# Sending tokens to slots: a routed expert layer that computes 13 of its 16 experts only for the tokens that chose them

## The chip, the cores and the metric

The kernel runs on one core of a Trainium2 chip. The metric is device time in microseconds (us) of one execution, taken as the median of several runs. The profile shown below is one execution recorded by the hardware profiler. All data are float32. TensorE is called PE in the profile (its weight loads PEld), VectorE DVE, ScalarE ACT, GpSimd POOL, and the engine that issues the ordinary DMAs SP.

## The reference, cut to what matters

Two transformer layers run over 1024 tokens of 256 channels. Each half of a layer is `x = x + layernorm(f(layernorm(x)))`; the four `f` are softmax attention, a mixture of 8 experts, a gated linear attention with 16 heads, and the mixture that is changed here:

```
def L1_ffn(x, gate_weight, gate_up_weights, down_weights, shared_gate_up, shared_down):
    # x: 1024 x 256; 16 experts of inner width 176; the shared one has 352
    scores = softmax(x @ gate_weight.T)
    topk_weight, topk_idx = top_k(scores, 4)
    y = 0
    for e in range(16):
        w_e = sum(where(topk_idx == e, topk_weight, 0), axis=-1)
        y += w_e[:, None] * glu(x, gate_up_weights[e], down_weights[e])
    return y + glu(x, shared_gate_up, shared_down)

def glu(x, gate_up, down):
    g, u = split(x @ gate_up.T, 2)
    return (silu(g) * u) @ down.T
```

A token has a non-zero weight for 4 of the 16 experts only. Counted with the reference on its own inputs, the 16 experts are chosen by 263, 231, 231, 261, 269, 237, 265, 251, 290, 273, 234, 236, 233, 246, 294 and 282 tokens.

## The kernel before

The whole network is one program. `Net.__init__` runs `attention0`, `experts0`, `attention1` and `experts1` one after the other. The residual `x` and the sum `acc` of the running half layer stay in SBUF by token (8 tiles of 128 tokens, `TT = 8`), and the normalised input `hT` stays there by channel (2 chunks of 128 channels by 1024 tokens). Weights come through a pool of two buffers, `wpool`; `load_next` issues the next group's DMAs on SP.

`experts1` treats all 16 experts and the shared one as a single layer with 16 x 176 + 352 = 3168 inner rows. These rows are cut into tiles of up to 128 (25 tiles), in groups `L1F`: first the shared expert's 3 tiles, then 22 tiles in groups of five (`FG1 = 5`). For each tile and each half of the tokens (512 of them) `gated` makes two products of two matmuls each (`pg` and `pu`, L803), ACT takes Silu of the one (L805), and DVE multiplies (L806) into `mid`. A tile of a routed expert is then multiplied by the weights of its tokens (`weigh`, L867). These weights lie along the free axis, so the routing weights are transposed (L771, L772), written to DRAM (L789) and read back as a broadcast over the partitions (L1407). `down` multiplies `mid` with the down weights, one matmul of 256 columns for each tile of tokens and each tile of rows (`po`, L821), and adds to `acc` (L829). After the last group `turn_out` normalises `acc`, adds `x` and sends the result out (L183 to L188, L314, L317, L318).

`router1` (L1435 to L1444) makes the routing weights for all 8 tiles of tokens at once, from logits of 16 matmuls (`pl`, L780). Which token chose which expert plays no part in how much is computed: every expert runs over all 1024 tokens, and a weight of zero removes what was not chosen.

The instructions are put in order when the program is built. The written order gives the priority, and each engine then runs its list strictly in that order; an instruction may be moved ahead of others that are not expected to be ready. `pinned` (`keep_in_program_order`) forbids that for single instructions. The last pieces of the previous half layer (the transposes of `h` into `hT`, L259 and L260) are kept in the list `todo` and run between the first tiles of `experts1` by `catch_up`.

Of the kernel before, what the change touches and what calls it, by code (L numbers as in the profile page):

```python
# [8 lines left out]

F32 = mybir.dt.float32  # L10
AF = mybir.ActivationFunctionType
ALU = mybir.AluOpType
# [3 lines left out]
P = 128  # L16
T = 1024
# [14 lines left out]
E1, F1, TOP1 = 16, 176, 4  # L32
FR = E1 * F1
FS = 2 * F1
FALL = FR + FS
FG1 = 5

L1F = [(FR, FS)] + [(lo, min(FG1 * P, FR - lo)) for lo in range(0, FR, FG1 * P)]

# [10 lines left out]
class Net:  # L50
    def __init__(self, ctx, tc, a, out):
# [39 lines left out]
        with tc.tile_pool(name="late", reuse_waits="tile", bufs=1) as late:  # L91
# [9 lines left out]
            self.experts0()  # L101
        self.attention1()
        self.experts1()

# [93 lines left out]
    def turning(self, ps, tp, acc=None):  # L198
# [41 lines left out]
        yield  # L240
        h = self.row.tile([P, 2, D], F32, tag="h2", name="h")
        for i, x in enumerate(xs):
# [95 lines left out]
    def normed0(self, tts):  # L338

        nc = self.nc
        n = len(tts)
        mv = self.mv0[:, tts[0] : tts[0] + n, :]
        for i, tt in enumerate(tts):
            st = self.small.tile([P, 6], F32, tag="st", name="st")
            nc.vector.bn_stats(st, self.x[:, tt, :])
            nc.vector.bn_aggr(mv[:, i, :], st)
        ve, rsx = (self.small.tile([P, n], F32, tag=t, name=t) for t in ("ve0", "rsx0"))
        nc.vector.tensor_scalar(ve, mv[:, :, 1], 1.0 + EPS, EPS * EPS, ALU.mult, ALU.add)  # L350
        nc.gpsimd.tensor_tensor(rsx, ve, self.nhalf[:, 0:n], ALU.pow)
        xns = []
        for i, tt in enumerate(tts):
            xn = self.row.tile([P, D], F32, tag="h", bufs=6, name="xn")
            nc.vector.tensor_scalar(
                xn, self.x[:, tt, :], mv[:, i, 0:1], rsx[:, i : i + 1], ALU.subtract, ALU.mult
            )
            xns.append((tt, xn))
        return xns, rsx
# [14 lines left out]
    def project0(self, tt, ps, qk, va, rotate):  # L374
# [12 lines left out]

        ra = self.row.tile([P, 2 * H, ROT], F32, tag="ra", bufs=2, name="ra")
        rb = self.row.tile([P, 2 * H, ROT], F32, tag="rb", bufs=2, name="rb")
        cos = self.rope[:, tt, 0, :].unsqueeze(1).to_broadcast([P, 2 * H, ROT])  # L390
# [4 lines left out]
        if rotate is not nc.vector:  # L395
            turn = self.row.tile([P, 2 * H, ROT], F32, tag="rc", bufs=2, name="rc")
            nc.scalar.copy(turn, src[:, :, 0:ROT])
# [7 lines left out]
    def attention0(self):  # L405
# [3 lines left out]
        QT = TT // 2  # L409
        with ExitStack() as ctx:  # L410
            big = ctx.enter_context(tc.tile_pool(name="a_big", reuse_waits="tile", bufs=1))
            qkp = ctx.enter_context(tc.tile_pool(name="a_qk", reuse_waits="tile", bufs=2))
# [394 lines left out]

    def down(self, ps, pieces, first, hf=None, then=None, apart=False):


        nc = self.nc
        begin, end = (0, TT) if hf is None else (hf * TT // 2, (hf + 1) * TT // 2)
        units = [list(range(tt, tt + 2)) for tt in range(begin, end, 2)]
        if apart:
            units[-1:] = [[tt] for tt in units[-1]]
        for tts in units:
# [15 lines left out]

    def experts(self, ps, tmp, midp, groups, route, weigh, then, join=False):


# [9 lines left out]
        def gates(half, some=slice(None)):  # L845
            g, tiles, hf, mid = half
            if join and (g, hf) == (0, 0):

                for part in (slice(0, HALF // 2), slice(HALF // 2, HALF)):
                    for i, (wg, wu, right, m, row) in enumerate(tiles):  # L850
                        self.gated(ps, tmp, wg, wu, mid[0:m, i, :], m, hf, part)
                    if part.start == 0:
                        self.catch_up(ps, 3)
                return
            for i, (wg, wu, right, m, row) in list(enumerate(tiles))[some]:
                self.gated(ps, tmp, wg, wu, mid[0:m, i, :], m, hf)
                self.catch_up(ps, 2)
                if g > 1:
                    weight(half, i)
# [9 lines left out]
        def down(*parts):  # L869
# [6 lines left out]
            last = g == len(groups) - 1  # L876
            self.down(ps, pieces, g == 0, hf, then if last else None, join and last and hf == 1)
            if hf == 1:
# [25 lines left out]
        for g in range(2, len(groups)):  # L904
            tiles = groups[g]()
            if join and g == 3:
                self.shifted()
            for hf in range(2):
                half = start(g, tiles, hf)
                if join and g >= len(groups) - 2 and (g, hf) != (len(groups) - 2, 0):  # L910
                    gates(half)
                    if g == len(groups) - 1:
                        down(behind.pop(0), half)
                    else:
                        behind.append(half)
                    continue
                if g == len(groups) - 1 and hf == 1:
# [103 lines left out]
    def attention1(self):  # L1021
# [3 lines left out]
        with ExitStack() as ctx:  # L1025
# [346 lines left out]
            for h in range(H):  # L1372
                ahead = enter(h + 1) if h + 1 < H else iter(())
                for _ in attend(h):
                    next(ahead, None)
                for _ in ahead:
                    pass


    def experts1(self):  # L1380
        nc, tc, a = self.nc, self.tc, self.a
        with ExitStack() as ctx:
            one = ctx.enter_context(tc.tile_pool(name="d_one", reuse_waits="tile", bufs=1))
            midp = ctx.enter_context(tc.tile_pool(name="d_mid", reuse_waits="tile", bufs=4))
            tmp = ctx.enter_context(tc.tile_pool(name="d_tmp", reuse_waits="tile", bufs=3))
            wp = ctx.enter_context(tc.tile_pool(name="d_w", reuse_waits="tile", bufs=7))
            ps = ctx.enter_context(tc.tile_pool(name="d_ps", reuse_waits="tile", bufs=8, space=PSUM))

            wr = one.tile([P, KC, E1], F32, name="wr")
            nc.sync.dma_start(out=wr, in_=a["e1_wrT"].rearrange("(k p) e -> p k e", p=P))  # L1390
            spreads = {}

            def route():
                w = self.router1(one, ps, wr)
                yield
                spreads["all"] = self.in_dram("w1", self.by_token(one, ps, w, E1), E1)
                yield

            def weigh(lo, m):

                if lo >= FR:
                    return None
                if lo not in spreads:
                    t = wp.tile([P, T], F32, tag="w", name="w")
                    for e in range(lo // F1, (lo + m - 1) // F1 + 1):
                        p0, p1 = max(e * F1 - lo, 0), min((e + 1) * F1 - lo, m)
                        nc.sync.dma_start(  # L1407
                            out=t[p0:p1, :], in_=spreads["all"][e, :].partition_broadcast(p1 - p0)
                        )
                    spreads[lo] = t  # L1410
                return spreads[lo]

            def group(g):
                gT, uT, dT = self.loaded.pop(0)
                tiles = []
                begin, rows = L1F[g]
                for i in range(-(-rows // P)):
# [6 lines left out]
                    ))  # L1424
                return tiles

            groups = [lambda g=g: group(g) for g in range(len(L1F))]
            self.experts(ps, tmp, midp, groups, route(), weigh, self.turn_out, True)

    def router1(self, one, ps, wr):  # L1430
        nc = self.nc
        sh = [P, TT, E1]
        pl = self.logits(ps, wr, E1)
        top = one.tile([P, TT, 1], F32, name="top")
        nc.vector.tensor_reduce(top, pl, AX.X, ALU.max)  # L1435
        w = one.tile(sh, F32, name="w")
        nc.vector.tensor_tensor(w, pl, top.to_broadcast(sh), ALU.subtract)
        nc.scalar.activation(w, w, AF.Exp)
        tot = one.tile([P, TT, 1], F32, name="tot")
        nc.vector.tensor_reduce(tot, w, AX.X, ALU.add)  # L1440
        nc.vector.reciprocal(tot, tot)
        nc.vector.tensor_tensor(w, w, tot.to_broadcast(sh), ALU.mult)
        chosen = self.first_k(one, w, E1, TOP1)
        nc.vector.tensor_tensor(w, w, chosen, ALU.mult)  # L1444
        return w

# [20 lines left out]
def layout(inputs):  # L1467
# [5 lines left out]
    def swap(v):  # L1473
        return v.transpose(0, 2, 1)

    def by_channel(v):
# [11 lines left out]
    )  # L1488
    gu, sgu = i["L1_ffn_gate_up_weights"], i["L1_ffn_shared_gate_up"]
    arrays = {  # L1490
        "x": i["L0_attn_X"].reshape(T, D), "cpack": cpack, "rope": _rope_table(),
# [8 lines left out]
        "e1_wrT": i["L1_ffn_gate_weight"].T,  # L1500
        "e1_gT": np.concatenate([gu[:, :F1].reshape(FR, D), sgu[:FS]], axis=0).T,
        "e1_uT": np.concatenate([gu[:, F1:].reshape(FR, D), sgu[FS:]], axis=0).T,
        "e1_dT": np.concatenate(
            [swap(i["L1_ffn_down_weights"]).reshape(FR, D), i["L1_ffn_shared_down"].T], axis=0
        ),
    }
# [18 lines left out]
```

## Time and profile before

| What | Value |
|---|---|
| Median of 3 runs | 1280.89 us (1280.16 to 1281.85) |
| The profiled execution's own time | 1274.77 us |
| Its span, first to last instruction | 1272.7 us |
| First matmul of `experts1` | 997.8 us into the span |
| Mean granted TensorE clock | 0.990 |

The profiled execution is 6.1 us faster than the median of the runs, and 2.07 us of its own time lie outside the span. In the page's lines on groups, the columns are line, engine, operation, output and inputs, shapes, and number of instructions, then busy time in us and mean duration in ns, then the idle time before them and what ended it. In answers on windows, each row is a stretch of the span with the busy time of every engine (and its number of instructions in brackets), the granted clock as a share of full speed, the share of the 16 DMA engines' time, and GB/s. "SPq" marks the issue of a DMA.

### The profile page before, as it was taken

What the parts mean: (1) busy time and instruction counts of PE and PEld (TensorE: products, weight loads), DVE (VectorE), ACT (ScalarE), POOL (GpSimd) and SP (SyncE); (2) the same over time, 40 slices, a digit from 0 to 9 for tenths busy, and PEclk for the clock granted to TensorE, in tenths of its full rate; (3) what the DMA queues carried; (4) which work ended last, traced back from release to release, by engine and by line L of the source; (5) the groups of instructions that cost most, each with busy time, mean ns of one, the idle gap of its engine ahead of it and who ended that gap; (6) DMA issues with size and microseconds to landing.
All of it is one profiled execution on the core that took longest, in us unless ns stands there. A gap on an engine that the chain in (4) does not pass through costs nothing. (4 is left out here: it accounts for less than half of the span.)

```text
span 1272.7 us, 15799 instructions
## 1 busy us (share of the span) xinstructions
PE 1214.0 (95%) x6152; PEld 727.1 (57%) x6152; DVE 732.0 (58%) x1646; ACT 501.0 (39%) x926; POOL 127.8 (10%) x118
## 2 busy tenths in 40 slices
PE   7999999999999997999999999999998899999997
PEld 4533333324456564567676776677677557555655
DVE  5876767732542355776777777768585633333234
ACT  4266665664310114444445454444544221121011
POOL 3100000000000001112111111121212200000001
PEclk9999999999899999999999999999999999999999
DMA  6000000000033012102030202120211106523000
GB/s 196 1 1 1 1 1 1 1 1 1 1 127 106 0 42 60 53 34 81 28 108 29 80 34 75 34 75 34 75 34 36 62 1 172 157 78 128 18 25 33
DMA packets 38922, 64.41 MB, mean 51 GB/s; under 512 B 4776, under 2 KB 28552, under 8 KB 38848
## 3 DMA queue, kind: packets, MB, share of 16 engines
q1 hardware_dynamic: 38848, 63.41, 15.8%
q8 instruction: 48, 0.79, 0.3%
q14 instruction: 26, 0.21, 0.1%
HBM read 62.12 MB, written 1.28 MB: 50 GB/s over the span
## 5 line engine op out<-in xcount | busy, mean ns | idle before, releaser
L481 DVE TENSOR_REDUCE pm<-sc 128x1 f32<-128x512 f32 x256 | 163.1, 684 | 64.5 <-PE sc L545 43.2
L806 DVE TENSOR_TENSOR mid<-sg,pu 128x512 f32<-128x512 f32 (+2 forms) x85 | 56.7, 667 | 194.1 <-PE pu L803 190.7
L805 ACT ACTIVATE sg<-pg 128x512 f32<-128x512 f32 (+2 forms) x85 | 49.4, 581 | 280.9 <-PE pg L803 280.9
L545 PE MATMUL sc<-qTm,kT 32*128 32x512 f32 x512 | 151.4, 643 | 1.9 <-ACT pe L563 1.9
L574 ACT ACTIVATE pe<-sc 128x512 f32<-128x512 f32 x216 | 117.7, 595 | 67.9 <-PE sc L545 47.3
L476 PE MATMUL sc<-kT,qT 32*128 32x512 f32 x512 | 136.3, 638 | 1.6 <-ACT qT L435 0.8
L1144 ACT ACTIVATE sn<-pt,shift,rs 128x128 f32<-128x128 f32 x256 | 93.5, 469 | 106.8 <-DVE shift L1140 106.8
L1104 PE MATMUL px<-hT,w_l1a 128*128 128x512 f32 x256 | 125.4, 602 | 5.4 <-DVE y L1096 5.1
L1096 DVE SCALAR_TENSOR_TENSOR y<-px,cp,y 128x1023 f32<-128x1023 f32 (+5 forms) x102 | 123.5, 1213 | 3.9 <-ACT y L1090 3.8
L803 PE MATMUL pg<-hT,w_l1f 128*128 128x512 f32 (+3 forms) x212 | 95.7, 574 | 2.1 <-ACT hT L260 2.1
L803 PE MATMUL pu<-hT,w_l1f 128*128 128x512 f32 (+3 forms) x212 | 95.4, 573 | 0.0
L829 DVE TENSOR_TENSOR acc<-acc,po 128x512 f32<-128x512 f32 (+1 forms) x55 | 37.2, 676 | 94.0 <-PE po L821 94.0
L821 PE MATMUL po<-w_l1f,mid 128*128 128x256 f32 (+1 forms) x400 | 87.6, 379 | 0.0
L821 PEld LDWEIGHTS po<-w_l1f,mid 128*128 128x128 f32 (+1 forms) x400 | 76.0, 190 | 13.5 <-issue 3.3
L1139 POOL TENSOR_TENSOR rs<-ve,nhalf 128x8 f32<-128x8 f32 x32 | 52.3, 1636 | 300.6 <-DVE ve L1138 245.9
L532 PE MATMUL po<-pe,va 128*32 128x256 f32 (+1 forms) x872 | 79.7, 433 | 1.3 <-ACT oT L537 0.8
L545 PEld LDWEIGHTS sc<-qTm,kT 32*128 32x128 f32 x512 | 49.6, 185 | 54.2 <-issue 38.5
L1208 PE MATMUL pg<-hT,w_l1a 128*128 128x512 f32 x128 | 62.0, 610 | 7.3 <-DVE og L1324 5.6
L803 PEld LDWEIGHTS pu<-hT,w_l1f 128*128 128x128 f32 (+1 forms) x212 | 40.6, 191 | 46.1 <-issue 45.0
L532 PEld LDWEIGHTS po<-pe,va 128*32 128x32 f32 x872 | 18.0, 108 | 85.0 <-issue 75.3
L803 PEld LDWEIGHTS pg<-hT,w_l1f 128*128 128x128 f32 (+1 forms) x212 | 40.1, 192 | 43.7 <-issue 39.8
L803 PE MATMUL pg<-hT,w_l0f 128*128 128x512 f32 x128 | 62.8, 612 | 0.0
(212 smaller groups left out, 1876.6 us busy)
## 6 DMA issues: line engine op xcount, KB each, us to landing
spread<-rows SPq DMA_DIRECT2D x32, 512.0 KB, 4.6
w<-w SPq DMA_DIRECT2D x16, 512.0 KB, 5.8
w_l1f<-in_e_gT SPq DMA_DIRECT2D x4, 640.0 KB, 4.0
w_l1f<-in_e_uT SPq DMA_DIRECT2D x4, 640.0 KB, 5.3
w_l1f<-in_e_dT SPq DMA_DIRECT2D x4, 640.0 KB, 7.0
w_l0f<-in_e_wg SPq DMA_DIRECT2D x4, 512.0 KB, 6.1
w_l0f<-in_e_wu SPq DMA_DIRECT2D x4, 512.0 KB, 7.2
w_l0f<-in_e_wd SPq DMA_DIRECT2D x4, 512.0 KB, 8.1
```

What stands on the lines that cost most here:

```text
L476: nc.tensor.matmul(sc, raw[r, tt * P : (tt + 1) * P], kT[r, g, half(kh)], start=True, stop=True,)
L481: nc.vector.tensor_reduce(pm[:, tt, 2 * pair + i, kh : kh + 1], sc, AX.X, ALU.max)
L532: nc.tensor.matmul(po[0][rows(j), c], va[:, st, g * G + j, :], pe[j // 2][:, j % 2, c], start=(st == 0), stop=(st == TT - 1 and c.stop == ...
L545: nc.tensor.matmul(sc, kT[rows(j), g, st * P : (st + 1) * P], qm[rows(j), :], start=True, stop=True,)
L574: nc.scalar.activation(pe[pair][:, i, :], sc, AF.Exp, scale=scale)
L803: nc.tensor.matmul(p, w(k), self.hT[:, k, c], start=(k == 0), stop=(k == KC - 1))
L806: nc.vector.tensor_tensor(mid, sg, pu, ALU.mult)
L821: nc.tensor.matmul(po[:, i, :], left[:, at * P : (at + 1) * P], right, start=(n == 0), stop=(n == len(pieces) - 1),)
L1096: nc.vector.scalar_tensor_tensor(y[:, at:hi], px[:, at - j : hi - j], column(cw + 4 * h + 3 - j), y[:, at:hi], ALU.mult, ALU.add,)
L1104: nc.tensor.matmul(px[:, c], w[:, k, hh * DK : (hh + 1) * DK], self.hT[:, k, c], start=(k == 0), stop=(k == KC - 1),)
L1144: nc.scalar.activation(sn[:, n, :], pts[n // 4][:, n % 4, :], AF.Identity, scale=rs[:, n : n + 1], bias=shift[:, n : n + 1],)
L1208: nc.tensor.matmul(pg, wg[:, k, hh * DK : (hh + 1) * DK], self.hT[:, k, c], start=(k == 0), stop=(k == KC - 1),)
```

## The change

The last three routed experts and the shared one keep the old form: `FD = 352 + 3 x 176 = 880` rows, 7 tiles instead of 25. They are called the dense part here. The other 13 (`SP1 = 13`) go through slots:

- `ways`, run before `attention1`, fills constants with POOL. `empty`, called once for each head of `attention1`, issues DMAs on SP that clear the first 336 rows of each expert's slots and a table of sums, both in DRAM: 13 of 357 KB and 11 of 128 KB.
- `routed(hf)` runs the router for one half of the tokens. It also counts, with matmuls against a triangle of ones (`earlier`) and a matrix of ones, how many earlier tokens chose the same expert, and makes from that the slot of each token in each expert. Then POOL issues, for each tile of 128 tokens and each of the token's 4 choices, an indirect DMA that writes the tokens' rows (256 channels, 13 weights and an index: 1088 bytes) to their slots. These are 16 DMAs for each half.
- `crowded` finds whether an expert was chosen by more than 336 tokens, and loads the answer into a register of every engine. `tc.If` takes `to_slots` if none was, and `to_all` otherwise, which computes the 13 experts for all tokens.
- `to_slots` reads, for each expert, its 336 rows from the slots (`fetch`), transposes them on PE (`turn`), makes the gated products with 336 columns (`middle`) and the down products with tokens on the partitions, scaled by the routing weight (`out`). It then sends the result with three indirect DMAs of 112 rows that add to the table of sums in DRAM. The adds of an expert wait for those of the expert before (`behind`). The weights come three experts at a time (`load`). At the end the sums are read back, added to `acc`, and `turn_out` runs.

The diff, cut to its core:

```diff
-L1F = [(FR, FS)] + [(lo, min(FG1 * P, FR - lo)) for lo in range(0, FR, FG1 * P)]
+SP1 = 13
+CP, CT = 112, 3
+CAP = CP * CT
+FD = FS + (E1 - SP1) * F1
+FG1 = 4
+L1F = [(lo, min(FG1 * P, FD - lo)) for lo in range(0, FD, FG1 * P)]
...
+        with tc.tile_pool(name="route", reuse_waits="tile", bufs=1) as self.route:
+            self.ways()
+            self.attention1()
+            self.experts1()
...
+                if h >= 1:
+                    self.empty(h - 1)
...
+            def routed(hf):
...
+                for i in range(N):
+                    for j in range(TOP1):
+                        tt = hf * N + i
+                        sent = nc.gpsimd.indirect_dma_start(
+                            out=self.slots[:, :],
+                            out_offset=bass.IndirectOffsetOnAxis(
+                                ap=place[:, tt, j : j + 1].bitcast(U32), axis=0
+                            ),
+                            in_=self.hrow[:, tt, :], in_offset=None,
+                            bounds_check=SLOTS - 1, oob_is_err=False,
+                        )
...
+            routed(0)
+            group(1)
+            for i in range(FG1, len(tiles)):
+                gates(i, 0)
+                self.catch_up(ps, 2)
+            self.catch_up(ps, len(self.todo))
+            routed(1)
+            for i in range(FG1):
+                gates(i, 1)
+            full = crowded()
+            spreads()
+            for i in range(FG1, len(tiles)):
+                gates(i, 1)
+            self.shifted()
...
+            def to_slots():
...
+                for i in range(2):
+                    load(i)
+                    fetch(i)
+                turn(0)
+                for e in range(SP1):
+                    if e + 1 < SP1:
+                        turn(e + 1)
+                    middle(e)
+                    if e > 0:
+                        out(e - 1)
+                    if e + 2 < SP1:
+                        fetch(e + 2)
+                    if e > 0:
+                        if e % S3 == 0 and (e // S3 + 1) * S3 < SP1 :
+                            load(e // S3 + 1)
+                out(SP1 - 1)
+                got = self.hT.rearrange("p k t -> p (k t)").rearrange("p (t d) -> p t d", d=D)
+                for tp in range(TT // 2):
+                    tts = [2 * tp, 2 * tp + 1]
+                    v = got[:, 2 * tp : 2 * tp + 2, :]
+                    read = nc.sync.dma_start(
+                        out=v, in_=self.sums[2 * tp * P : (2 * tp + 2) * P, :].rearrange("(t p) d -> p t d", p=P)
+                    )
+                    behind(read, added[SP1 - 1])
+                    acc = self.acc[:, 2 * tp : 2 * tp + 2, :]
+                    nc.vector.tensor_tensor(acc, acc, v, ALU.add)
+                    self.turn_out(ps, tts)
...
+            with tc.If(full == 0, preferred_fallthrough_block=True) as fits:
+                to_slots()
+            with fits.Else():
+                to_all()
```

Inside `out(e)`, the part that sends:

```diff
+                    for i in range(CT):
+                        sent = nc.gpsimd.indirect_dma_start(
+                            out=self.sums[:, :],
+                            out_offset=bass.IndirectOffsetOnAxis(
+                                ap=xs[:, i, XID : XID + 1].bitcast(U32), axis=0
+                            ),
+                            in_=ys[:, i, :], in_offset=None, bounds_check=TRASH - 1,
+                            compute_op=ALU.add,
+                        )
...
+                        behind(sent, added.get(e - 1, ()))
```

The rows fetched for an expert (`xs`) have three buffers, their transposes (`xT`) two, and the weights of three experts (`sw`) two.

## The prediction

> **What bounds the kernel now.** I read the busy table first, then the stage around the change by windows and by groups, then the chain of waits for the pace of a matmul.
>
> ```profile
> PE 1214.0 (95%) x6152; PEld 727.1 (57%) x6152; DVE 732.0 (58%) x1646; ACT 501.0 (39%) x926; POOL 127.8 (10%) x118
> q8 instruction: 48, 0.79, 0.3%
> ```
>
> PE is the bound over the whole span. For the stage (busy us of PE, PEld, DVE, ACT, POOL; clock; DMA share; GB/s):
>
> ```profile
> 997.80:1265.50 267.70, 266.18 (x876) 162.47 (x876) 93.47 (x191) 47.87 (x85) 7.01 (x13) 0.99 0.26 76
> 1065.00:1070.00 5.00, 5.00 (x25) 4.38 (x24) 2.58 (x4) 1.01 (x2) 0.00 (x0) 1.00 1.04 224
> 8.00:16.00 8.00, 7.45 (x21) 4.32 (x22) 4.81 (x20) 2.47 (x8) 2.99 (x4) 1.00 1.00 308
> 500.00:510.00 10.00, 4.86 (x12) 2.17 (x12) 5.78 (x10) 4.57 (x6) 0.00 (x0) 0.83 0.37 94
> ```
>
> From the first gate matmul to the last down matmul PE lacks 1.5 us. POOL is free. The 16 DMA engines are full at 224 GB/s in the broadcasts, at 308 in plain loads. The pace, from the chain (start, length, items; each matmul has its load):
>
> ```profile
> 1030.30 3.48 PE pl L780 x32
> 1122.60 1.72 PE pu L803 x4
> 1124.32 8.63 PE po L821 x40
> ```
>
> A matmul of 512 columns takes 0.86 us (1.68 ns a column), one of 256 takes 0.431, and a short one 0.217, whatever its width. What ends the kernel and what the DMAs cost:
>
> ```profile
> 1267.22 0.43 DVE L183 BATCH_NORM_STATS2 st<-acc 128x6 f32<-128x256 f32 x1
> 1269.64 0.42 DVE L317 TENSOR_TENSOR x<-x,acc 128x256 f32<-128x256 f32 x1 [0.67 <-ACT acc L314]
> x<-in_x SPq DMA_DIRECT2D x4, 256.0 KB, 3.3
> out_y<-x SPq DMA_DIRECT2D x8, 128.0 KB, 1.7
> spread<-rows SPq DMA_DIRECT2D x32, 512.0 KB, 4.6
> ```
>
> And a row on order: DVE ran an L806 inside the router's chain, which is written ahead of it.
>
> ```profile
> 1037.04 0.41 DVE L755 TENSOR_TENSOR_SCAN nth<-within,eq 128x128 f32<-128x128 f32 x1
> 1037.59 0.69 DVE L806 TENSOR_TENSOR mid<-sg,pu 128x512 f32<-128x512 f32 x1
> 1038.19 0.29 DVE L759 TENSOR_TENSOR nth<-nth,more 128x128 f32<-128x128 f32 x1
> ```
>
> So waiting steps are passed by ready ones; I use this for PE's order below.
>
> **The change part by part.** *PE, before:* 25 tiles x 2 halves x 4 x 0.86 = 172.0; downs 8 x 25 x 0.431 = 86.3; logits 3.5, transposes 3.5: 265.3, which is the 266.2 of the window. *PE, dense part after:* gates 7 x 8 x 0.86 = 48.2; downs 8 x 7 x 0.431 = 24.2; logits 3.5; transposes 3.5; the counts, 9 matmuls for slots and 2 for the limit, 2.4. Sum 81.8. *PE, one expert in slots:* 6 transposes 1.3, 6 gate matmuls of 336 columns 6 x 0.565 = 3.4, 6 down matmuls 2.6: 7.3, times 13 is 94.6. PE's work falls from 266 to 176. The rest of the sum is what is given back.
>
> *Dense part, waits.* The 1.5 us stay. The register load makes every engine wait for `over`; no row shows one. Below, 0 (PE has queued work); above, 4; the smallest loads land in 1.6 to 2.6 us, so I take 2. Behind it on PE stand the last three tiles' gates, which nothing else needs early. The broadcasts of the routing weights: before, from the issue of the write (1056.0) to the fifth tile's weighting (1073.4) took 17.4 us, hidden behind unweighted work. Now 2.1 MB instead of 2.6 go the same way (14 us, and 2 for transposes and copies), and PE has 10.3 us of gates to cover it and one more of unweighted downs: 5 us of wait. The dense part ends at 997.8 + 81.8 + 1.5 + 2 + 5 = 1088; 1 for the branch makes 1089. The two routers' chains on DVE (22 small instructions of 0.2 to 0.4 each, about 6 us) and their four table loads on ACT (1.28 each) lie beside gates; without that cover they would cost some 9 us a half.
>
> *POOL's indirect DMAs.* The trace has none. Their issue time X is bounded below by SP's issue of a plain DMA (0.37 to 0.46 us), above by twice POOL's L1139 (1.64 us for 8 columns), that is 3.3[...]. Nearest in kind is a small POOL instruction: 0.2 (memset) to 0.7 (pow). The Trainium skill (DMA: Bandwidth & Descriptors, section on latency and other measured facts) puts the first byte of a POOL-issued DMA at about 1 us against 0.6 for SP's. I take 1.2. For the landing L of an add: below 1.7 (out_y), above 1.7 + 3.3 (a read ahead of the write). The same page's section on the anatomy of one DMA has 2.0 us fixed; with it the sum would be about 6 us shorter. I take 3.0. The 32 sends: half 0 from about 1025, half 1 from about 1045, 16 x 1.2 each, landed by about 1067; the first fetch (4 us, between 3.3 and 4.6) is in at 1071. PE reaches it at 1089: hidden, up to X of about 2.3. On POOL behind the sends stand only the register load and the adds; on SP the first fetch holds up `load(1)`, wanted three experts later.
>
> *The slots' loop.* Three limits for one expert: PE, 7.3; the chain of adds, 3X + L + 0.3 = 6.9; and the ring of three row buffers, since the fetch of expert e + 3 waits for the adds of e: fetch 4.3, transposes 1.3, copy 0.6, gates 3.4, Silu and product 1.2, downs 2.6, scaling 0.6, adds 6.6, together 20.6 for three experts, 6.9. Limits so close cannot be met at once: a step that comes back finds PE in another expert's step, on average half of a 1.3 to 3.4 us step. I add 0.8: 8.1 for an expert, 105.5 for 13, and 0.6 + 6.6 until the last adds have landed: 113. DVE (1.5) and ACT (2.6 per expert, from 0.45 and 0.38 a piece) are covered. DMA moves 1.3 to 1.7 MB per expert, 160 to 210 GB/s, within the 308; but 1.9 MB of weights stand three times ahead of fetches on SP's queue (6 us at 308, mostly covered): 4. Adds end at 1089 + 113 + 4 = 1206.
>
> *The tail.* Before, 7.2 us followed the last down matmul. Now nothing of the output can be normalised before the last add: read back 3.4, then four pairs of tiles on DVE, 3.1 each (L829 0.69, two each of 0.43, 0.18 and 0.43, two of 0.16) = 12.4, 1.5 of POOL and ACT for the last pair, 2.6 to the end of the output. 19.9: 1226. All engines then jump over `to_all`. The trace has no jump; instruction fetches are DMAs (q8), and the smallest land in 1.6 to 2.6: bounds 0 and 4, I take 2.
>
> *Attention.* 24 clearing DMAs on SP lie at 0.4 us of issue each in a queue that is mostly idle; 8 of 16 scans already wait for `spread`, 7.9 us in all, with PE losing 1.0 of it. `ways` is a dozen POOL constants (about 5 us) before POOL has work. Together 0 to 10; I take 2. The edits of pools and of `h`'s place cost nothing: no instruction is added.
>
> Sum: 1226 + 2 + 2 = 1230, against the span's 1272.7: 42.7 less, 1232 in its own time. The median stands 6.1 above that execution, so 1280.9 - 42.7 = 1238.
>
> **A rule against the change.** The window 500 to 510 shows a clock of 0.83 where PE was busy 4.86 of 10 us. The skill (TensorE: Matmul & The Clock Gate, The HAM clock gate) says that an idle window of about 3.4 us halves the clock until about as long a busy one. My gap per expert is 0.8 us: by rule nothing. If the loop takes 11 us, gaps reach 3.7, and the rule would put up to 3.6 us on each expert's 7.3 (up to 47 in all), the row's 0.83 only 1.5 (19). I take nothing in the main case, and let it widen the upper end.
>
> **The rivals.**
> *POOL's chain of adds becomes the bound* (slower). Each expert then costs 3X + L, the span is 1089 + 14 + 13(3X + L) + 28. Break-even is 3X + L = 10.9: X = 2.6 with L = 3, 2.3 with L = 4. At X = 3, L = 4 it is 1300 (run 1308). For: neither is in the trace, and POOL's rows are slow for their size. Against: the middle of the bounds is below. A PE order kept as written (turn of e + 2 ahead of middle of e + 1) ends there too: a ring of some 33 us for three of which only two overlap, over 14 us an expert; the L806 row speaks against it.
> *A middling POOL*: X = 2, L = 3 to 4: chain and ring 9 to 10, adds end 18 to 31 later: run 1256 to 1272.
> *PE stays the bound*: X = 0.6, L = 2, no broadcast wait: 104 for 113, 5 and 4 us less elsewhere: run 1220.
> *The branch goes to all tokens*: 13 x 4 x 10 x 0.431 = 224 after the dense part, run about 1330. The counts of the reference's own router on its inputs reach 290 in the first 13 experts, under the 336: 0.01.
>
> **How the numbers follow.** About the forecast (1225 to 1255) 0.56, PE-bound 0.08, middling POOL 0.13: 0.77 faster. Within 0.2% (2.6 us, about what a measurement can tell from no change) 0.02. Slower 0.21: POOL's chain 0.14, order and clock 0.06, branch 0.01. The range leaves out some 0.06 below 1214 and 0.13 above 1292.
>
> **What would show it.** In the profile after: PE's first transposes of slot rows near 1089; PE about 1125 us busy; POOL's issues about 1.2 us apart; adds of one expert about 8.5 us after those of the one before; 20 to 24 us between the last down matmul's adds and the end. PE idle over 3 us an expert, waiting on a fetch that waits on adds, would make the forecast wrong, as would POOL issues over 2.3 us.

## The result and the profile after

| Kernel | Median (lowest to highest), us | Ratio to before (95% interval) |
|---|---|---|
| before | 1280.5 (1279.2 to 1281.9) | |
| changed | 1369.0 (1367.7 to 1369.9) | 1.069 (1.067 to 1.071) |

The change makes the kernel 88 us slower; the forecast had it 43 us faster, with a range that ended at 1292. The profiled execution after has a span of 1365.8 us and a mean clock of 0.924, against 1272.7 and 0.990. The busy table and the granted clock in 40 slices, of the changed kernel:

```profile
PE 1150.0 (84%) x5996; PEld 704.3 (52%) x5996; DVE 699.0 (51%) x1634; ACT 516.7 (38%) x972; POOL 220.7 (16%) x208
PEclk9999999999999999999999999999987996666685
```

PE's work did fall, from 1214.0 to 1150.0. It is now busy for 84% of the span, and the clock stands at 0.6 in most of the last slices: PE has less to do and waits. Where, the windows show (length; busy us and instructions of PE, PEld, DVE, ACT, POOL; clock; DMA share; GB/s). The first row is the dense part (first gate to last down matmul), the second the slots from 1.8 us behind the first add (1119.7) to the landing of the last, the third what follows the last add:

```profile
1001.60:1107.80 106.20, 90.25 (x330) 61.74 (x331) 32.06 (x112) 25.12 (x46) 35.97 (x41) 0.89 0.35 101
1121.50:1345.20 223.70, 100.12 (x336) 70.05 (x336) 16.21 (x32) 29.94 (x68) 55.33 (x38) 0.68 0.29 57
1345.20:1365.80 20.60, 0.00 (x0) 0.00 (x0) 9.68 (x36) 4.32 (x8) 3.29 (x4) 0.50 0.32 103
```

Against the forecast's sum, in spans: the first gate stands at 1001.6 for 999.8 (1.8 more); the dense part and the entry of the branch take 106.2 for 91.2 (15.0 more); the slots, to the landing of the last adds at 1345.2, take 237.4 for 117 (120.4 more); tail and jump take 20.6 for 21.9 (1.3 less). Together that is 1365.8 for 1230. So there are two things to explain, and the large one is in the slots. The waits from 990 us on, and the same of SP's own queue from 1060 (engine and line, what it waited for: us in total, times, longest):

```profile
POOL sums L1728 <- ACT ys L1723: 201.7, 12, 46.3
PE pt L1694 <- DMA xs<-slots: 109.8, 10, 12.7
SPq L1687 <- DMA sums<-ys,xs: 177.7, 11, 38.4
```

POOL waits for scaled rows, so it is not the bound. PE waits ten times, 11 us each, for the fetch of an expert's rows, and SP holds that fetch back until adds have landed. One period, in order of time (start, length, instruction, idle time before it and what ended that; a few rows between left out):

```profile
1180.61 1.45 POOL L1728 DMA_INDIRECT sums<-ys,xs  x1 [16.33 <-ACT ys L1723]
1182.37 1.46 POOL L1728 DMA_INDIRECT sums<-ys,xs  x1 [0.30 <-issue]
1184.13 1.46 POOL L1728 DMA_INDIRECT sums<-ys,xs  x1 [0.30 <-issue]
1187.81 0.30 SPq L1687 DMA_DIRECT2D xs<-slots  x1
1191.14 1.35 PE L1694 MATMUL pt<-ident,xs 112*128 112x112 f32 x6 [10.46 <-DMA xs<-slots]
1192.29 5.61 PE L1673 MATMUL pe<-xT,sw 128*128 128x336 f32 x12
...
1197.74 0.59 PE L1718 MATMUL po<-sw,mid 128*112 128x256 f32 x2
...
1199.66 1.34 ACT L1723 ACTIVATE ys<-po,xs 112x256 f32<-112x256 f32 x3 [1.28 <-PE po L1718]
...
1200.41 1.45 POOL L1728 DMA_INDIRECT sums<-ys,xs  x1 [14.83 <-ACT ys L1723]
```

Read it as one chain without a gap: adds until they have landed 7.20 us (1180.61 to 1187.81), fetch 3.33, transposes 1.15, gates 5.45, downs and scaling 2.67, and then the next expert's adds: 19.80. The three kinds of work on PE belong to three experts. In the code, each turn of the loop runs `turn(e + 1)`, `middle(e)`, `out(e - 1)`, and PE follows that order. `turn(e + 1)` needs the rows of e + 1; with three row buffers their fetch needs the adds of e - 2; and `out(e - 1)`, which feeds the next adds, stands on PE behind the waiting `turn(e + 1)`. So the ring goes round once for every expert, not once for three: 12 us an expert over the forecast for the ten experts that wait, nearly all of the 120.4.

### The profile page after: what moved, and what is told of

It reads as the page before. It is cut to its first block, busy times and chain, and to the rows that moved or that the text cites. A ratio compares the mean times of both kernels' runs of the same rounds, so it can differ in the third digit from the quotient of the medians.

```text
span 1365.8 us, 15745 instructions
## 1 busy us (share of the span) xinstructions
PE 1150.0 (84%) x5996; PEld 704.3 (52%) x5996; DVE 699.0 (51%) x1634; ACT 516.7 (38%) x972; POOL 220.7 (16%) x208
## 5 line engine op out<-in xcount | busy, mean ns | idle before, releaser
L1694 PE MATMUL pt<-ident,xs 112*128 112x112 f32 x78 | 15.6, 366 | 109.8 <-DMA xs<-slots 109.8
L825 DVE TENSOR_TENSOR mid<-sg,pu 128x512 f32<-128x512 f32 (+2 forms) x50 | 32.1, 643 | 123.9 <-PE pu L822 94.9
L1728 POOL DMA_INDIRECT sums<-ys,xs x39 | 56.9, 1459 | 212.6 <-ACT ys L1723 201.7
L1701 DVE COPY xT<-pt 128x336 f32<-128x336 f32 x13 | 6.6, 508 | 159.5 <-PE pt L1694 159.5
L824 ACT ACTIVATE sg<-pg 128x512 f32<-128x512 f32 (+2 forms) x50 | 27.7, 561 | 126.7 <-PE pg L822 122.7
L231 POOL TENSOR_TENSOR rss<-ve,nhalf 128x2 f32<-128x2 f32 x12 | 8.4, 698 | 407.7 <-DVE ve L230 402.8
L1694 PEld LDWEIGHTS pt<-ident,xs 112*128 112x128 f32 x78 | 12.3, 203 | 114.0 <-issue 113.7
L1673 PE MATMUL pe<-xT,sw 128*128 128x336 f32 (+1 forms) x156 | 65.0, 583 | 0.4 <-ACT xT L1699 0.4
L1172 PE MATMUL pv<-w_l1a,hT 128*128 128x256 f32 x256 | 60.2, 384 | 1.3 <-DVE state L1306 0.7
```

What stands on the lines that cost most here:

```text
L1673: nc.tensor.matmul(p, wg[:, k, lo : lo + m], right(k), start=(k == 0), stop=(k == KC - 1))
L1728: sent = nc.gpsimd.indirect_dma_start(out=self.sums[:, :], out_offset=bass.IndirectOffsetOnAxis(ap=xs[:, i, XID : XID + 1].bitcast(U32), a ...
```

## The experiments

The theory to test (A) is this ring: three buffers, and a turn that waits ahead of work that is ready. Its rivals are that the adds themselves, each behind those of the expert before on one table, set the pace (B), or that the low clock does (C).

**Five row buffers for three** (two of them lie in `hrow`, which nothing reads any more by then):

```diff
+ring = [xsp.tile([CP, CT, XR], F32, name=f"xs_{i}") for i in range(3)]
+ring += [self.hrow[0:CP, CT * i : CT * i + CT, :] for i in range(2)]
-    rows[e] = xsp.tile([CP, CT, XR], F32, tag="xs", name="xs")
+    rows[e] = ring[e % len(ring)]
```

> The changed kernel with five buffers for the fetched rows instead of three (two of them lie in hrow, which is free by then); nothing else. Theory A (the ring: a fetch waits for the adds of three experts before, and PE stands at that fetch's transposes): an expert falls from 20 us to the chain of adds, 3 x 1.76 + 3.5 = 8.8 us; 13 of them 115 us instead of 225, so some 1259 us instead of 1369. Theory B (the chain of adds on POOL is the bound by itself): no change, 1369. Theory C (PE's granted clock of 0.68 is the bound): PE needs 7.3 / 0.68 = 10.7 us an expert, some 1283 us, and the clock stays low.

Measured: 1251.9 us (1248.6 to 1254.6), ratio 0.979 (0.976 to 0.982): 117 us less than the changed kernel. Its waits and a window of its slots:

```profile
PE pt L1696 <- DMA xs<-slots: 7.6, 4, 3.0
PE pt L1696 <- DMA hrow<-slots: 1.1, 1, 1.1
POOL sums L1730 <- DMA sums<-ys,xs: 10.6, 3, 4.9
1121.00:1215.00 94.00, 77.47 (x339) 56.04 (x337) 16.21 (x32) 30.36 (x71) 49.90 (x35) 0.97 0.58 120
```

PE's 109.8 us of waiting for fetches are down to 8.7 (the second row is the two buffers in `hrow`), its clock is 0.97, and the first adds of two experts lie 8.3 us apart (from 1121.5 for the first expert to 1220.8 for the last, over 12). The expectation's chain of adds of 8.8 counts the third issue twice: from the first add to the landing of the third it is the 7.2 read above.

**Three buffers, other order**: the turn behind the work that is ready.

```diff
 for e in range(SP1):
-    if e + 1 < SP1:
-        turn(e + 1)
     middle(e)
     if e > 0:
         out(e - 1)
+    if e + 1 < SP1:
+        turn(e + 1)
```

> The changed kernel with three buffers as before, but turn(e + 1) written behind middle(e) and out(e - 1) instead of ahead of them. Theory A: the wait for the fetch (10.6 us from the end of one out to the rows landed) then lies beside one other expert's steps: 10.6 + 9 us cover two experts, about 10 us each, so some 1276 us. Theory B: 1369. Theory C: 1369, since PE's work and its pauses stay.

Measured: 1266.5 us (1262.6 to 1274.6), ratio 0.9925 (0.989 to 0.996). The instructions and bytes are those of the changed kernel, only their order differs, and 102 us are gone. What is left of the wait:

```profile
PE pt L1694 <- DMA xs<-slots: 18.2, 7, 5.2
```

**Two tables for the sums**, for even and for odd experts, with three buffers and the old order. The adds of an expert then wait for those of two experts before; at the end both tables are added.

```diff
-out=self.sums[:, :],
+out=(self.sums if e % 2 == 0 else self.sums2)[:, :],
...
-behind(sent, added.get(e - 1, ()))
+behind(sent, added.get(e - 2, ()))
```

> The changed kernel with two tables of sums: experts of even and of odd number add to different tables, so that the adds of an expert wait only for those of two experts before; both tables are read and added at the end. Theory A: the adds waited for nothing but their own rows (3.0 us in all), so an expert stays at 20 us; the second table costs 2 to 4 us at the end: 1372. Theory B: the chain is cut in two, an expert falls to some 10 us: 1260.

Measured: 1367.0 us (1363.3 to 1370.8), ratio 1.069 (1.065 to 1.073), as the changed kernel. PE waits as before:

```profile
PE pt L1698 <- DMA xs<-slots: 109.3, 10, 12.5
```

So the order of the adds does not set the pace while the ring does.

**PE kept busy**: 11 matmuls of 512 columns that nothing uses, ahead of each of the ten turns of the changed kernel that wait.

```diff
+    if 1 < e and e + 1 < SP1:
+        spare = ps.tile([P, HALF], F32, tag="b1", name="spare")
+        for _ in range(11):
+            self.pinned(nc.tensor.matmul(
+                spare, self.ident, self.hT[:, 0, 0:HALF], start=True, stop=True))
     if e + 1 < SP1:
         turn(e + 1)
```

> The changed kernel with 11 matmuls of 512 columns (9.5 us at full clock), whose result is not used, put between out(e - 1) and turn(e + 1), where PE otherwise waits 10.6 us for the fetch. They keep PE busy and depend on nothing. Theory A: the ring stays, only PE's own steps in it get faster with the clock (gates 5.4 to 3.4 us): about 2 us an expert less, some 1345 us. Theory C (the clock is the cause): 9 us an expert less, some 1260 us. Theory B: 1369.

Measured: 1346.5 us (1344.8 to 1348.5), ratio 1.053 (1.050 to 1.056). The same window of the changed kernel and of this one:

```profile
1121.00:1280.00 159.00, 71.45 (x231) 49.62 (x232) 11.65 (x23) 19.81 (x45) 33.76 (x24) 0.67 0.28 60
```

```profile
1121.00:1280.00 159.00, 144.85 (x458) 79.98 (x457) 13.17 (x26) 22.60 (x52) 39.28 (x27) 0.99 0.32 69
```

The same steps of one expert in this kernel:

```profile
1186.88 0.77 PE L1694 MATMUL pt<-ident,xs 112*128 112x112 f32 x6 [1.15 <-DMA xs<-slots]
1187.48 3.57 PE L1673 MATMUL pe<-xT,sw 128*128 128x336 f32 x12
1190.88 0.59 PE L1718 MATMUL po<-sw,mid 128*112 128x256 f32 x2
```

The 110 useless matmuls make the kernel 22 us faster. With the clock at 0.99 for 0.67, an expert's transposes take 0.60 for 1.15 and its gates 3.40 for 5.45; the rest of the ring is as it was. The clock is a cost on top of the ring, not the ring: 67 us above before remain.

**Five buffers and two tables together.**

> Five buffers for the fetched rows (as e1_bufs) and two tables of sums (as e3_tables) together. If, with the ring loosened, the chain of adds is the next bound (3 x 1.76 + 3.5 = 8.8 us against PE's 7.3), the second table, worth nothing alone, now gives 0.9 to 1.5 us an expert, less 2 to 4 us for reading it: some 1240 us against e1_bufs' 1252. If PE or the fetches behind the weights on SP's queue bind in e1_bufs, nothing or a loss: 1252 to 1256.

Measured: 1229.9 us (1227.2 to 1232.9), ratio 0.9625 (0.959 to 0.966). With the ring open, the second table, worth nothing alone, is worth 22 us: the first adds of two experts now lie 6.7 us apart, near PE's own 6.6 (shown below).

**The dense part.** There PE waited at `pr` (L1527) for the router's chain on VectorE, once in each half's router:

```profile
PE pr L1527 <- DVE nth L1517: 6.7, 1, 6.7
PE pr L1527 <- DVE chosen L1523: 3.6, 1, 3.6
```

To test whether that is the 15 us, the router is cut in two, and gates are written between the logits and `pr`:

```diff
 nc.vector.tensor_tensor(c, c, eq, ALU.add)
+yield
 pr = ps.tile(sh, F32, tag="b1", name="pr")
...
-routed(0)
+first, second = routed(0), routed(1)
+next(first)
...
     gates(i, 0)
     self.catch_up(ps, 2)
+    if i == FG1 + 1:
+        next(first, None)
```

(and likewise for the second half).

> The changed kernel (three buffers, one table) with only the router written in two parts: its slot counts (pr) follow two gate tiles later instead of at once, for both halves of the tokens. Theory A: the dense part's excess of some 16 us over the forecast is PE standing at pr for the DVE chain (3.6 + 6.7 us) and the lower clock after it (0.76 of full in that stretch): 8 to 14 us less, some 1357 us. Rival: the broadcast of the routing weights ends the dense part and takes the gain back: 1366 to 1369.

Measured: 1374.4 us (1371.5 to 1375.4), ratio 1.075 (1.071 to 1.079): 5 us slower than the changed kernel, where a gain was expected. The theory as stated fell. The waits at `pr` are gone, and others have come. All of ACT's rows in a stretch of its timeline:

```profile
1039.88 0.60 ACT L824 ACTIVATE sg<-pg 128x512 f32<-128x512 f32 x1 [1.56 <-issue]
1047.81 0.60 ACT L824 ACTIVATE sg<-pg 128x512 f32<-128x512 f32 x1 [7.33 <-remote]
1057.61 0.60 ACT L824 ACTIVATE sg<-pg 128x512 f32<-128x512 f32 x1 [9.20 <-remote]
1076.56 1.05 ACT L1595 COPY wT<-pt 3x512 f32<-3x512 f32 x2 [18.35 <-remote]
```

The transposes that the last row reads ended on PE at 1050.7; the copy starts 26 us later. On VectorE a row of the same stretch, whose input ended on PE at 1049.8, starts 8.3 us after the row before it:

```profile
1075.11 0.17 DVE L1576 TENSOR_REDUCE most<-pc 128x1 f32<-128x13 f32 x1 [8.34 <-remote]
```

In this stretch POOL issues the 32 scatters of rows one behind the other, 0.30 us apart, until 1072.3. The changed kernel has the same thing, smaller: of its two copies of wT one starts at 1066.04 and the other, whose input was ready by 1066.3, at 1071.00. The same cut in the kernel with five buffers and two tables also cost time:

> Five buffers, two tables and the router in two parts. If the three effects add: some 1229 us. If the earlier dense part only waits longer for the slots' sends or for the weights: as e4_bufs_tables.

Measured: 1237.8 us (1234.7 to 1243.5), ratio 0.968 (0.964 to 0.971), 8 us above the same without the cut. With the late turn as well:

> As e7_all, with turn(e + 1) written behind middle(e) and out(e - 1). If what is left of PE's waits in the slots are late fetches: 3 to 6 us less than e7_all, some 1225 us. If PE has no such waits left: the same as e7_all, or 1 to 2 us more, since a transpose is then copied with nothing beside it.

Measured: 1241.3 us (1238.8 to 1243.7), ratio 0.972 (0.968 to 0.975), no gain: with five buffers the order no longer decides.

**The scatters.** If they hold ScalarE and VectorE up, leaving them out must shorten the dense part (the experts then work on the blank rows in the slots). In the changed kernel:

```diff
-sent = nc.gpsimd.indirect_dma_start(
-    out=self.slots[:, :],
...
-    in_=self.hrow[:, tt, :], in_offset=None,
-    bounds_check=SLOTS - 1, oob_is_err=False,
-)
+pass
```

> The changed kernel without the 32 scatters of rows to slots (L1554); left out is just that: the experts then take the blank rows that lie in the slots, whose adds go to the spare rows of the table, with the same number of instructions and transfers. In the trace of the changed kernel ScalarE and VectorE start late while POOL issues the scatters: the second copy of wT stands at 1071.00, 4.4 us after the first, and the gates after it wait until 1076, 2.5 us after the last scatter. Theory A (the scatters hold the other engines up): the last down matmul of the dense part, at 1107.9, comes some 4 to 8 us earlier, at 1100 to 1104, and the time falls from 1369 to about 1362, because the slots keep their 19.5 us an expert. Theory B (those waits are dependences of the router and of the read of the counts): the end of the dense part stays within 2 us of 1107.9 and the time within 3 us of 1369.

Measured: 1356.3 us (1355.3 to 1356.8), ratio 1.061 (1.058 to 1.064). The dense part takes 96.4 us (1001.2 to 1097.6) for 106.2, a little more gained than expected. In the other kernels with the whole router and the scatters on POOL the same part took 103.7 to 109.4, so the 9.8 is good to about 3. In the kernel with the router cut in two:

> The kernel with the router in two parts, without the 32 scatters (the same part is left out as in the run before). With the scatters its trace shows PE without a wait until 1056, then ACT's waits of 9.2 and 18.4 us and VectorE's of 12.6 and 8.3, which all end between 1057 and 1077, and the dense part's end at 1113.3. Theory A (the scatters hold the others up): these waits go, PE runs on, and the dense part ends at 1088 to 1094, some 20 us earlier; the time falls from 1374 to about 1352. Theory B (the order of the engines' instructions makes them): the end of the dense part stays within 3 us of 1113 and the time within 4 us of 1374.

Measured: 1347.0 us (1343.1 to 1349.2), ratio 1.054 (1.051 to 1.058). The dense part takes 84.0 us (1001.1 to 1085.1) for 112.0. So without scatters the cut of the router is worth 12.4 us, as its theory had it; with them, the scatters cost 28 us and eat it. Next, the same number of writes and bytes, issued as plain writes by SP and not by POOL:

```diff
-sent = nc.gpsimd.indirect_dma_start(
-    out=self.slots[:, :],
...
+sent = nc.sync.dma_start(
+    out=self.slots[j * T + tt * P : j * T + (tt + 1) * P, :], in_=self.hrow[:, tt, :])
```

> The changed kernel with each of the 32 scatters written as a plain write on the SP queue: 128 rows of 1088 B to one stretch of the same table, in the same order, so that the bytes and rows moved are the same and POOL issues none; the rows no longer go to the experts that were chosen. If the scatters hold other engines up by their traffic (packets in the 16 DMA engines), the dense part ends at 1106 to 1110 as in the changed kernel; if by being issued on POOL, it ends at 1100 to 1104 as expected without them. The time is 1369 for the first and about 1362 for the second.

Measured: 1358.0 us (1356.7 to 1359.6), ratio 1.062 (1.059 to 1.065). The dense part takes 96.7 us, as with no scatter at all. The ends of the dense part, shown by PE's first transposes of slot rows behind it, in the changed kernel, without scatters, with the cut router and no scatters, and with the plain writes:

```profile
1107.86 1.31 PE L1694 MATMUL pt<-ident,xs 112*128 112x112 f32 x12
1097.63 1.31 PE L1685 MATMUL pt<-ident,xs 112*128 112x112 f32 x12
1085.13 1.31 PE L1691 MATMUL pt<-ident,xs 112*128 112x112 f32 x12
1100.00 1.31 PE L1690 MATMUL pt<-ident,xs 112*128 112x112 f32 x12
```

(The last kernel's first gate stands at 1003.3, 1.7 us later than the changed kernel's.) So it is not the amount of traffic that holds the others up, but something in its being indirect and issued by POOL. These two were not told apart: no kernel issued plain writes on POOL. Last, the kernel with five buffers, two tables and the cut router, with a pause behind each scatter:

```diff
 sent = nc.gpsimd.indirect_dma_start(
     out=self.slots[:, :],
...
 tc.add_to_no_dep_group("sent", sent.ins)
+self.pinned(nc.gpsimd.memset(self.rest, 0.0))
```

> The kernel with five row buffers, two tables and the router in two parts, with one small POOL memset of a spare tile (256 columns; rows of 128 and 336 columns take 0.21 and 0.39 us, so about 0.3) behind every one of the 32 scatters. That kernel without the memsets ran 1238 and its dense part ended at 1116.4, with the scatters from 1033.9 to 1073.9. Theory A (ScalarE and VectorE are held because the scatters are issued back to back, and a pause between two lets them start): the waits at sg, mid and wT fall under 4 us each, the dense part ends at 1095 to 1108, and the time is 1218 to 1230. Theory B (each scatter delays the others by the same amount, pause or no pause, or they wait for the end of the row of scatters): the scatters last 12 to 20 us longer, the dense part ends at 1116 to 1130 and the time is 1238 to 1252.

Measured: **1214.1 us** (1213.4 to 1216.3), ratio **0.949** (0.947 to 0.951), the fastest of all, 24 us less than without the pauses and under what was expected. Rows of its timeline, and the window of its dense part:

```profile
1047.14 0.97 POOL L1560 DMA_INDIRECT slots<-hrow,place  x1 [0.16 <-issue]
1048.11 0.33 POOL L1570 MEMSET rest<- 128x256 f32 x1
1048.60 0.97 POOL L1560 DMA_INDIRECT slots<-hrow,place  x1 [0.17 <-issue]
1048.72 1.03 PE L1600 MATMUL pt<-ident,w 128*3 128x128 f32 x8
1049.36 1.05 ACT L1601 COPY wT<-pt 3x512 f32<-3x512 f32 x2 [1.92 <-PE pt L1600]
1000.10:1084.70 84.60, 83.64 (x331) 58.13 (x332) 32.91 (x114) 25.36 (x46) 47.68 (x73) 0.97 0.34 107
```

The scatters now come 1.46 us apart and not 1.28, and last 7 us longer; yet wT is copied 0.64 us after its transposes begin, and the dense part takes 84.6 us, near the 84.0 without any scatter. PE, ScalarE and VectorE run the same instructions in the same order through the dense part with and without the pauses, so it is not a new order that helps. The longer row of scatters may show up once: PE waits 4.2 us for the second fetch of slot rows. The pauses were tried in this kernel only, not in the changed one.

## Why the prediction was wrong

- **The step that failed**: "So waiting steps are passed by ready ones; I use this for PE's order below." From one pair of rows on VectorE, a rule for PE was made. In `to_slots` PE runs exactly the order written (why the build moved nothing there, no run shows), and a waiting `turn(e + 1)` holds `middle(e)` and `out(e - 1)` behind it. That turns "together 20.6 for three experts, 6.9" into 19.8 for each. The loop of "8.1 an expert" took 20.1 for the first ten (first adds at 1119.7, and at 1321.1 ten experts later). The order alone, undone, gives back 102 us; the buffers alone give back 117.
- **The rival that came true** was in the text, as a PE order kept as written, "over 14 us an expert", with a share of the 0.06 for order and clock. Its mechanism was right and its size too small: no two of the ring's turns overlapped. It was weighed by that one row, when the loop's text and the buffer count already spelled out the cycle. The text's own sign of failure, PE idle for over 3 us an expert on a fetch that waits on adds, is what the waits show.
- **The pace without the ring**: 8.1 forecast, 8.3 measured with five buffers, but in part by luck. The 8.1 was PE's 7.3 and 0.8 for steps that meet. What paced the five buffers was the chain of adds, since a second table alone brought the pace to 6.7. PE's own part is smaller than forecast, as rows of one expert and the start of the next in the last kernel show:

```profile
1101.83 0.74 PE L1708 MATMUL pt<-ident,hrow 112*128 112x112 f32 x6
1102.40 3.57 PE L1685 MATMUL pe<-xT,sw 128*128 128x336 f32 x12
1105.81 0.60 PE L1732 MATMUL po<-sw,mid 128*112 128x256 f32 x2
1108.40 0.74 PE L1708 MATMUL pt<-ident,hrow 112*128 112x112 f32 x6
```

That is 6.6 an expert. The six transposes take 0.57 and not 1.3: "a short one 0.217, whatever its width" was read from the router's logits alone, and a row of transposes in the kernel before has eight in 0.87, 0.109 each:

```profile
1054.47 0.87 PE pt L771 x8
```

- **X and L**: POOL's add takes 1.46 and 0.30 to the next, so 1.76 for the 1.2 taken. L, counted behind the third issue, was 1.9 (7.2 less 3 x 1.76) for 3.0; the 2.0 that the prediction set beside it was nearer. The 1 us to the first byte no trace here shows. The chain of adds is 7.2 for 6.6, far from the break-even of 10.9: POOL was not the bound of the changed kernel. A scatter takes 0.98 and 0.30, near the 1.2.
- **The clock**: "gap per expert 0.8 us: by rule nothing." The gaps were 10 to 13 us. Weighed for a loop of 11 us, the rule of the Trainium skill (TensorE: Matmul & The Clock Gate, The HAM clock gate) gave up to 47 us for 13 experts, 3.6 each, and the row at 0.83 gave 19, 1.5 each; the matmuls that kept PE awake recovered 22 over ten experts, 2.2 each. The measured price lies between the two. That the row's 19 is near the 22 is luck: the clock was 0.68 and not 0.83.
- **The dense part**, 15.0 us over. PE's own 81.8 is near the 84.0 and 84.6 of the two kernels without these waits. Two terms were put at nothing. VectorE's chains "lie beside gates": with the router whole, PE waited 10.3 us at `pr` (7.2 without scatters), the same mistake on order, and worth 12.4 once nothing else was in the way. The scatters were costed by their own end ("hidden, up to X of about 2.3"), and hold other engines up for 9.8. So 106.2 is 84.0 and 12.4 and 9.8. The waits that were allowed for (2 for the register, 5 for the broadcast) hide part of this miss; once both causes are gone, the broadcast's wait is under 1.
- **Tail, branch and attention**: 20.6 for 21.9; PE's first transposes follow the last down matmul without a gap, so the branch has no visible price there; attention cost 3.8 for 2 in this trace. The first gate stands between 1000.1 and 1004.3 in the others, so this term is no better known than that.
- **The idea** of the change held. With its waits removed, the routed kernel runs in 1214, below the 1238 forecast, but with four further edits, none of which was in the forecast.

## What to carry to other kernels

In a software pipeline with a ring of buffers, write out the cycle: what frees a buffer, and what stands in program order between the step that waits for the fetch and the step that frees it. If a waiting step stands ahead of ready ones on an in-order engine, every turn pays the whole round trip; move it behind them or add buffers before pricing anything else. That an engine passed a waiting step once shows an order that was built so at that place, not a rule for another loop. A long row of indirect DMAs on POOL can cost the other engines time even where nobody waits for its data; a short pause between two, tried here in one kernel, can be worth trying.

## What the runs showed of the hardware that was not expected

- While POOL issues indirect DMAs back to back, ScalarE and VectorE start late on work that has no visible dependence on them: by up to 18.4 us on ScalarE in the trace shown, and 9.8 and 28.0 us of the dense part in two kernels. Without the DMAs, or with plain writes of as many bytes by SP, this is gone, and so it is with a 0.33 us memset behind each. By what path they are held is not shown: the profile says only "remote" or "issue" for these waits.
- An indirect add of 112 rows of 1 KB occupies POOL for 1.46 us and lands some 3.6 us after its issue begins (1184.13 to 1187.81, when SP's fetch behind it goes out); a scatter of 128 rows of 1088 B occupies it for 0.98. Between two there are 0.30 us.
- With PE busy for 45% of the slots' window (100.1 of 223.7 us), its mean clock there was 0.68.
